# Four-layer graph network on one Trainium2 core: the order of work in the layer 0 edge loop

## The chip, the cores and the metric

The kernel runs on one core of one Trainium2 chip. Its time is the device time of one execution, in microseconds. The engines are TensorE (PE, with its weight loads as PEld), VectorE (DVE), ScalarE (ACT), GpSimd (POOL) and SyncE (SP). Each works through its own instructions in the order in which the program issues them, and waits for others by semaphores.

## The reference

Nodes N = 4096, features D = 512, edges E = 65536, everything in float32. Four layers follow each other; each one normalises the rows, takes the ReLU, lets a graph operation work on them and adds the result to x. The change lies in layer 0, an attention layer with 8 heads of 64 features over the set of distinct edges and self loops:

```python
h = jnp.einsum('nc,hcf->hnf', x, W)
e = s_src[:, :, None] + s_dst[:, None, :]      # one score of each node as source, one as destination
e = jnp.where(e > 0, e, ALPHA * e)
e = jnp.where(adj[None, :, :], e, NEG_INF)
att = jax.nn.softmax(e, axis=-1)
out = jnp.einsum('hij,hjf->hif', att, h)       # then concatenated over heads, softmax over axis 1
```

Layers 1 to 3 (a normalised sum over edges, a message network, another sum over edges) are not touched.

## The kernel before

Layer 0 first sorts the edges by source and projects all rows to `htab` (512 features and 8 scores per node). The function `attend` then walks over the sorted edges in `groups` = 64 groups of `GT` = 8 tiles of 128 edges. For every group it

- gathers 8 tiles of rows of `htab` with 8 indirect DMAs on POOL (`fetch`, three groups ahead, four buffers `rows`);
- makes one-hot matrices of the edges' sources on DVE (`one_hots`, line 414, one instruction for 8 tiles);
- turns these with 8 PE transposes into two PSUM tiles `t_ps` (`turn`, line 635), which ACT copies to `oh_t` (`turned`, line 643), while ACT (line 647) and DVE (line 648) blend the node parts of the two blocks that the group's sources can lie in into `of`;
- spreads these parts to the edges with 8 small PE products into `e_ps` (`source_parts`, line 656);
- makes the scores on DVE (`scores`, lines 662 to 668), their exponent on ACT (line 669), the weights on DVE (`weights`, line 676, into the PSUM tile `both_ps`) and a copy of the weights on ACT into the last columns of `rows` (line 677);
- weighs the rows pair by pair: 6 heads on DVE (`weigh`, line 690, one instruction for two tiles) and the last 2 heads on ACT (`weigh_last`, line 684, four instructions for two tiles);
- sums the weighed rows with the one-hots on PE (`add_up`, line 696; the trace shows 8 products for two tiles) into `sum_ps`, and one step later adds the sums to two blocks of `acc` on DVE (`keep`, line 431, two instructions).

The block numbers that `keep` and `turned` need are read into a register by the engine that uses them (`block_of`, line 425). In the trace such a read is a TENSOR_LOAD and a few register operations on the engine's sequencer (rows of "DVEq" and "ACTq").

Beside the groups run the blocks: when the sources have passed 128 nodes, the class `Block` finishes these rows (softmax, residual, layer norm, the product with layer 1's weights, line 408) in 13 small steps. `PLAN` says for each step how many groups after the block's end and at which named place of the loop it is issued. A block ends every two groups, so the steps of the loop alternate. In an odd step a block's `share`, `spread`, `variance`, `roots`, `sharpen`, `multiply` (8 PE products, line 408) and `put` are issued; in an even one `exponent` (ACT, line 730), `add` (DVE, lines 734 to 739), `normal`, `turn` (4 PE transposes, line 770), `turned` (ACT copy, line 774) and `store`.

PE, DVE, ACT and POOL keep the written order here (`tc.manual_schedule`), so the loop body below is each engine's queue. PSUM is full: two `sum_ps` of two banks, two `t_ps`, one `e_ps` and one `both_ps`. A group's two turned tiles and the block's turned tile or product share the two `t_ps` in turn.

Of the kernel before, what the change touches and what calls it, by code (L numbers as in the profile page):

```python
# [11 lines left out]
BF16 = mybir.dt.bfloat16  # L12
F32R = mybir.dt.float32r
I32 = mybir.dt.int32
AF = mybir.ActivationFunctionType
# [5 lines left out]
P = 128  # L21
# [13 lines left out]
def kernel(  # L35
# [23 lines left out]
    nc = tc.nc  # L59
    N, D = x.shape  # L60
    E, DE = edge_attr.shape
    H, _, F = w0.shape
# [45 lines left out]
    s_loc = src_pool.tile([P, W], F32, name="s_loc")  # L108
    s_new = src_pool.tile([P, W], F32, name="s_new")
    s_bi = src_pool.tile([1, 2, NW], I32, name="s_bi")  # L110
    s_half = src_pool.tile([P, 2, NW], F32, name="s_half")
# [299 lines left out]
    def one_hots(pool, loc, t0, n, bufs=None, ids=None, dtype=F32):  # L411

        oh = pool.tile([P, n, P], dtype, name="oh", bufs=bufs)
        nc.vector.tensor_tensor(oh, (row_i if ids is None else ids).unsqueeze(1).to_broadcast([P, n, P]),  # L414
                                loc[:, t0:t0 + n].unsqueeze(2).to_broadcast([P, n, P]), op=OP.is_equal)
        return oh
# [7 lines left out]
    def block_of(eng, bi, t):  # L424
        return eng.value_load(bi[:, t:t + 1], min_val=0, max_val=NB - 1)
# [163 lines left out]
    node3 = node_pool.tile([P, NB, 3, 2 * H], BF16, name="node3")  # L589
# [9 lines left out]
    GT = 8  # L599
# [4 lines left out]
    def attend(ctx):  # L604
        if True:
            ep = ctx.enter_context(tc.tile_pool(name="edge", bufs=2))
# [4 lines left out]
            ids_ps = both_ps[:, :P]  # L611
# [8 lines left out]
            def at(g):  # L620
                return g * GT
# [7 lines left out]
            def turn(oh):  # L629

                made = []
                for j in range(0, GT, 4):
                    t_ps = eps.tile([P, 4, P], F32, name="t_ps")
                    for k in range(4):
                        nc.tensor.transpose(t_ps[:, k, :], oh[:, j + k, :], ident)
                    made.append(t_ps)
                return made

            def turned(g, made):

                oh_t = ep.tile([P, GT, P], BF16, name="oh_t")
                for j, t_ps in enumerate(made):
                    nc.scalar.copy(oh_t[:, 4 * j:4 * j + 4, :], t_ps)
                of = ep.tile([P, 2, 3 * 2 * H], BF16, name="of")
                near = [node3[:, ds(block_of(e, s_bi[:, k, :], g), 1)].rearrange("p b k c -> p (b k c)")
                        for k, e in enumerate((nc.scalar, nc.vector))]
                nc.scalar.activation(of[:, 0, :], near[0], AF.Copy, scale=s_half[:, 0, g:g + 1])
                nc.vector.scalar_tensor_tensor(of[:, 1, :], near[1], s_half[:, 1, g:g + 1], of[:, 0, :],
                                               op0=OP.mult, op1=OP.add)
                return oh_t, of[:, 1, :]  # L650

            def source_parts(oh_t, of):

                e_ps = eps.tile([P, GT, 3, 2 * H], F32, name="e_ps", bufs=1)
                for j in range(GT):
                    nc.tensor.matmul(e_ps[:, j].rearrange("p k c -> p (k c)"), oh_t[:, j, :],
                                     of, start=True, stop=True)
                return e_ps

            def scores(rows, e_ps):  # L660
                near = ep.tile([P, GT, 2 * H], F32, name="near")
                nc.vector.reduce_sum(near, e_ps.rearrange("p t k c -> p t c k"), axis=AX.X)
                u = ep.tile([P, GT, H], F32, name="u")
                nc.vector.tensor_add(u, near[:, :, :H], rows[:, :, D:D + H])
                nc.vector.scalar_tensor_tensor(u, u, 0.2, u, op0=OP.mult, op1=OP.max)
                nc.vector.tensor_sub(u, u, near[:, :, H:])

                nc.vector.tensor_scalar(u, u, SAFE_RANGE + 10.0, None, op0=OP.min)
                nc.scalar.activation(u, u, AF.Exp)
                nc.scalar.copy(rows[:, :, D + H:], one2.unsqueeze(1).to_broadcast([P, GT, 2]))  # L670
                return u
# [7 lines left out]
            def weigh_last(j, rows):  # L679

                two = rows[:, j:j + 2]
                for k in range(2):
                    for h in range(VH, H):
                        nc.scalar.activation(two[:, k, h * F:(h + 1) * F], two[:, k, h * F:(h + 1) * F], AF.Copy,
                                             scale=two[:, k, D + h:D + h + 1])

            def weigh(g, j, rows):

                part = rows[:, j:j + 2, :VH * F].rearrange("p t (h f) -> p t h f", h=VH)
                nc.vector.tensor_mul(part, part,  # L690
                                     w_ps[:, g % 2, j:j + 2, :VH].unsqueeze(3).to_broadcast([P, 2, VH, F]))

            def add_up(j, rows, oh, ps):
                for k in range(2):
                    for c in range(2):
                        nc.tensor.matmul(ps[:, c, :HW], oh[:, j + k, :], rows[:, j + k, c * HW:(c + 1) * HW],  # L696
                                         start=j + k == 0, stop=j + k == GT - 1)
# [6 lines left out]
            class Block:  # L704
# [78 lines left out]
                def store(self):  # L783
                    nc.sync.dma_start(ytab[self.b * P:(self.b + 1) * P, :], self.row)

            PLAN = {"share": (0, "end"), "exponent": (1, "turned"), "add": (1, "end"), "spread": (2, "first"),
                    "variance": (2, "summed"), "roots": (2, "turned"), "sharpen": (2, "end"), "normal": (3, "first"),
                    "turn": (3, "between"), "turned": (3, "weighed"), "multiply": (4, "between"), "put": (4, "end"),
                    "store": (5, "summed")}
            begun = {}  # L790

            def blocks(g, place):

                for b in range(NB):
                    since = g - min(2 * b + 3, groups)
                    for step, when in PLAN.items():
                        if when == (since, place):
                            if step == "share":
                                begun[b] = Block(b)
                            getattr(begun[b], step)()  # L800
                            if step == "store":
                                del begun[b]

            rows, ohs, sums = {}, {}, {}
            for g in range(-3, groups + 6):
                now = lambda k: 0 <= k < groups
                if now(g + 3):
                    rows[g + 3] = fetch(g + 3)
                if now(g + 1):
                    made = turn(ohs[g + 1])  # L810
                if now(g):
                    sums[g] = eps.tile([P, 2, D], F32, name="sum_ps")
                    weigh(g, 0, rows[g])
                    add_up(0, rows[g], ohs[g], sums[g])
                    weigh_last(2, rows[g])
                    weigh(g, 2, rows[g])
                blocks(g, "first")
                if now(g - 1):
                    keep(g - 1, sums.pop(g - 1))
                    del rows[g - 1], ohs[g - 1]  # L820
                blocks(g, "summed")
                if now(g + 1):
                    parts = turned(g + 1, made)
                blocks(g, "turned")
                if now(g):
                    add_up(2, rows[g], ohs[g], sums[g])
                    weigh_last(4, rows[g])
                    weigh(g, 4, rows[g])
                if now(g + 2):
                    ohs[g + 2] = one_hots(ep, s_loc, at(g + 2), GT, 3, ids_ps)  # L830
                if now(g + 1):
                    e_ps = source_parts(*parts)
                if now(g):
                    add_up(4, rows[g], ohs[g], sums[g])
                blocks(g, "between")
                if now(g + 1):
                    u = scores(rows[g + 1], e_ps)
                if now(g):
                    weigh_last(6, rows[g])
                    weigh(g, 6, rows[g])  # L840
                blocks(g, "weighed")
                if now(g):
                    add_up(6, rows[g], ohs[g], sums[g])
                if now(g + 1):
                    weights(g + 1, rows[g + 1], u)
                    weigh_last(0, rows[g + 1])
                blocks(g, "end")

    one2 = node_pool.tile([P, 2], F32, name="one2")
    nc.vector.memset(one2, 1.0)  # L850
    attend()
    l0_pool.close()

# [173 lines left out]
    with tc.tile_pool(name="between", bufs=1) as bp, tc.tile_pool(name="between_ps", bufs=1, space=PSUM) as bps, \  # L1027
            tc.manual_schedule(engines=ENGINES):
        between = Between(bp, bps)
# [538 lines left out]
```

## Time and profile before

| | |
|---|---|
| time, median of 4 runs | 5419.7 us (5417.04 to 5427.41) |
| the profiled execution's own time | 5421.66 us |
| its span | 5419.9 us, granted TensorE clock 0.982 |
| PE, DVE, ACT, POOL busy over the span | 94%, 65%, 62%, 54% |
| layer 0 edge loop, first to last start of line 696 on PE | 256.7 to 926.6 us |
| one-hot instruction of one group (line 414, DVE) | 1.22 us, 64 of them |
| weigh instruction (line 690, DVE) | 0.95 us, 256 of them |

A row of a timeline is: start, duration, engine, line, operation, output and inputs, shape, number of instructions merged, and in brackets the idle time before the first of them with what ended it. Durations overlap on one engine, since the next instruction starts before the last one has drained, so the cost of an instruction in a full queue is the distance to the next start. A row of the waits is: who waited for whom, microseconds in total, times, the longest. A row of windows has the busy microseconds of PE, PEld, DVE, ACT and POOL with their instructions, the granted clock, the DMA share and the rate.

### The profile page before, as it was taken

The numbers are of one execution on the slowest core, as the hardware profiler recorded it, in microseconds if no ns is written. First come the engines' busy times: TensorE is split into PE (matmuls) and PEld (weight loads), VectorE is DVE, ScalarE is ACT, GpSimd is POOL, SyncE is SP. The second block draws the span as 40 slices with busy tenths as digits, with TensorE's granted clock in tenths as the row PEclk, the third lists the DMA queues.
The fourth block names the chain that finished last, engine by engine and source line by source line (L and its number), as shares of the span: only waits on it lengthen the run. The fifth ranks groups of instructions, "written<-read, shape, count | busy, mean of one in ns | idle before, by whom it ended". The sixth has DMA issues, their size and how long they took to land.

```text
span 5419.9 us, 56747 instructions
## 1 busy us (share of the span) xinstructions
PE 5093.7 (94%) x17274; PEld 2742.0 (51%) x17274; DVE 3526.8 (65%) x5843; ACT 3368.4 (62%) x5157; POOL 2910.4 (54%) x2604
## 2 busy tenths in 40 slices
PE   7799999799997999999999999999999899988887
PEld 4477776344443555555555555555555666522222
DVE  8689997333334777777777777777777466622333
ACT  1267776344445888888888888888888433333433
POOL 0177774777765555555555555555553111167776
PEclk9899999899998999999999999999999899999999
DMA  3388885888885555555555555555553211167787
GB/s 107 105 237 251 247 244 170 264 262 265 260 254 134 119 113 113 114 116 116 114 114 114 114 114 114 113 113 115 116 115 63 86 68 66 58 207 210 237 252 224
DMA packets 345929, 842.26 MB, mean 155 GB/s; under 512 B 61072, under 2 KB 77456, under 8 KB 345616
## 3 DMA queue, kind: packets, MB, share of 16 engines
q0 software_dynamic: 237568, 673.35, 50.0%
q1 hardware_dynamic: 108048, 165.19, 8.9%
q8 instruction: 141, 2.31, 0.2%
q14 instruction: 172, 1.41, 0.1%
HBM read 753.14 MB, written 85.20 MB: 155 GB/s over the span
## 4 chain that ended last, share of the span: by engine, by line
PE 77%; DMA 8%; POOL 6%; DVE 5%; issue 3%; ACT 1%; DVEq 0%; SPq 0%; POOLq 0%; ACTq 0%
PE m_ps L408 32%; PE sum_ps L887 9%; DMA g<-ztab,d_src 5%; PE small_ps L1084 4%; PE small_ps L1111 4%; PE o_ps L408 4%; PE tr_ps L1091 4%; PE sum_ps L696 4%; PE u_ps L1276 4%; PE pq_ps L985 4%; POOL g L419 4%; POOL rows L419 2%; DMA rows<-htab,s_dst 2%; PE t_ps L408 1%; PE tr_ps L1074 1%
## 5 line engine op out<-in xcount | busy, mean ns | idle before, releaser
L408 PE MATMUL m_ps<-w_sb,h_t 128*128 128x512 f32 x4096 | 1821.1, 592 | 0.5 <-ACT h_t L1093 0.5
L408 PEld LDWEIGHTS m_ps<-w_sb,h_t 128*128 128x128 f32 x4096 | 757.5, 190 | 809.6 <-issue 798.1
L887 PE MATMUL sum_ps<-g,oh 128*128 128x512 f32 x2048 | 1023.7, 617 | 143.7 <-DMA g<-ztab,d_src 92.5
L419 POOL DMA_INDIRECT pg<-ptab,d_src x512 | 497.6, 972 | 994.3 <-ACT h_t L1093 817.9
L1067 POOL DMA_INDIRECT pg<-qtab,d_dst x512 | 870.5, 1700 | 159.3 <-issue 153.2
L887 PEld LDWEIGHTS sum_ps<-g,oh 128*128 128x128 f32 x2048 | 357.7, 191 | 750.6 <-issue 343.3
L419 POOL DMA_INDIRECT rows<-htab,s_dst x512 | 491.9, 961 | 402.6 <-issue 371.2
L419 POOL DMA_INDIRECT g<-ztab,d_src x512 | 485.9, 949 | 240.7 <-issue 118.8
L419 POOL DMA_INDIRECT g<-ytab,s_dst x512 | 487.0, 951 | 234.1 <-issue 124.8
L1093 ACT COPY h_t<-tr_ps 128x512 f32<-128x512 f32 x512 | 275.2, 589 | 429.6 <-PE tr_ps L1091 429.4
L696 PE MATMUL sum_ps<-rows,oh 128*128 128x261 f32 x2048 | 495.1, 389 | 26.9 <-DVE rows L690 26.8
L431 DVE SCALAR_TENSOR_TENSOR acc<-sum_ps,d_half,acc 128x512 f32 x256 | 192.4, 751 | 444.0 <-PE sum_ps L887 418.5
L1143 DVE TENSOR_TENSOR pg<-pg,small_ps 128x512 f32<-128x512 f32 x512 | 318.3, 682 | 189.9 <-PE small_ps L1084 152.8
L696 PEld LDWEIGHTS sum_ps<-rows,oh 128*128 128x128 f32 x2048 | 376.6, 190 | 104.8 <-DVE rows L690 37.8
L431 DVE SCALAR_TENSOR_TENSOR acc<-sum_ps,s_half,acc 128x522 f32 (+1 forms) x256 | 193.1, 754 | 335.6 <-PE sum_ps L887 300.8
L1111 PE MATMUL small_ps<-parts,oh 128*128 128x512 f32 x1024 | 310.9, 446 | 13.4 <-DVE oh L414 13.4
L1105 DVE TENSOR_TENSOR parts<-z,parts 128x1024 fp32r<-128x1024 f32 x256 | 313.6, 1225 | 8.9
L1091 PEld LDWEIGHTS tr_ps<-ident,pg 128*128 128x128 f32 x2048 | 240.3, 141 | 145.5 <-issue 145.5
L1180 DVE TENSOR_TENSOR pg<-pg,qg 128x1024 f32<-128x1024 f32 x256 | 301.3, 1219 | 0.7 <-ACT qg L1177 0.7
L431 DVE SCALAR_TENSOR_TENSOR acc<-small_ps,d_half,acc 128x512 f32 x256 | 192.4, 752 | 161.4 <-PE small_ps L1111 152.5
L1267 POOL TENSOR_TENSOR h_sb<-h_sb,b_bc 128x1024 f32<-128x1024 f32 x16 | 38.1, 2382 | 453.9 <-PE tr L1251 430.2
L1091 PE MATMUL tr_ps<-ident,pg 128*128 128x128 f32 x2048 | 266.3, 273 | 10.4 <-DVE pg L1180 10.4
(281 smaller groups left out, 8047.7 us busy)
## 6 DMA issues: line engine op xcount, KB each, us to landing
eg<-in_edge_attr_dram SPq DMA_DIRECT2D x128, 128.0 KB, 2.6
xt<-in_x_dram SPq DMA_DIRECT2D x8, 1024.0 KB, 5.5
htab<-acc SPq DMA_DIRECT2D x32, 256.0 KB, 2.0
x_row<-in_x_dram SPq DMA_DIRECT2D x32, 256.0 KB, 4.3
rows<-htab,s_dst POOLq DMA_INDIRECT x512, 3.8
x<-x_row SPq DMA_DIRECT2D x32, 256.0 KB, 3.7
ytab<-acc SPq DMA_DIRECT2D x32, 256.0 KB, 4.4
x_mid<-x SPq DMA_DIRECT2D x32, 256.0 KB, 5.3
```

Source lines behind the costliest of these rows:

```text
L408: nc.tensor.matmul(ps, h_t[:, k, :], w_sb[:, k0 + k, :], start=start and k == 0, stop=stop and k == KC - 1)
L419: nc.gpsimd.indirect_dma_start(out=dst_ap, out_offset=None, in_=table, in_offset=bass.IndirectOffsetOnAxis(ap=idx, axis=0))
L431: nc.vector.scalar_tensor_tensor(at, ps, half[:, k, i:i + 1], at, op0=OP.mult, op1=OP.add)
L696: nc.tensor.matmul(ps[:, c, :HW], oh[:, j + k, :], rows[:, j + k, c * HW:(c + 1) * HW], start=j + k == 0, stop=j + k == GT - 1)
L887: nc.tensor.matmul(ps, oh[:, j, :], g[:, j, :], start=i % per == 0 and j == 0, stop=i % per == per - 1 and j == U - 1)
L1067: nc.gpsimd.indirect_dma_start(out=pg[:, j, :], out_offset=None, in_=qtab, in_offset=bass.IndirectOffsetOnAxis(ap=d_dst[:, t:t + 1], axis= ...
L1091: nc.tensor.transpose(h_ps[:, k, :], h[:, j, k * P:(k + 1) * P], ident)
L1093: nc.scalar.copy(h_t, h_ps)
L1105: nc.vector.tensor_sub(parts[:, 1], m, parts[:, 0].bitcast(F32))
L1111: nc.tensor.matmul(ps, oh[:, j, :], parts[j // 2][:, k, j % 2, :], start=j == 0 and k == 0, stop=j == U - 1 and k == 1)
L1143: nc.vector.tensor_add(nxt[:, j], nxt[:, j], ps)
L1180: nc.vector.tensor_mul(h[i][:, half], h[i][:, half], qg[:, half])
```

## The change

The one-hots are made, turned and copied two groups ahead instead of one, at the start of a step; the ACT half of the blend becomes a function of its own, issued before the copies; `source_parts` goes to the end of the step, two groups ahead. The first two pairs of the next group are weighed at the end of the step, the last two pairs of the group in its own step, so that `add_up(0)` and `add_up(2)` stand together at the start. `keep` goes behind the blocks' PE work. The one-hots get a fourth buffer. Two entries of `PLAN` move.

```diff
+            def near_scale(g):
+                of = ep.tile([P, 2, 3 * 2 * H], BF16, name="of")
+                near = node3[:, ds(block_of(nc.scalar, s_bi[:, 0, :], g), 1)].rearrange("p b k c -> p (b k c)")
+                nc.scalar.activation(of[:, 0, :], near, AF.Copy, scale=s_half[:, 0, g:g + 1])
+                return of
-            def turned(g, made):
+            def turned(g, made, of):
...
-                nc.scalar.activation(of[:, 0, :], near[0], AF.Copy, scale=s_half[:, 0, g:g + 1])
-                nc.vector.scalar_tensor_tensor(of[:, 1, :], near[1], s_half[:, 1, g:g + 1], of[:, 0, :],
+                near = node3[:, ds(block_of(nc.vector, s_bi[:, 1, :], g), 1)].rearrange("p b k c -> p (b k c)")
+                nc.vector.scalar_tensor_tensor(of[:, 1, :], near, s_half[:, 1, g:g + 1], of[:, 0, :],
...
-                    "variance": (2, "summed"), ... "turned": (3, "weighed"),
+                    "variance": (2, "weighed"), ... "turned": (3, "turned"),
...
-                if now(g + 1):
-                    made = turn(ohs[g + 1])
                 if now(g):
                     sums[g] = eps.tile([P, 2, D], F32, name="sum_ps")
-                    weigh(g, 0, rows[g])
                     add_up(0, rows[g], ohs[g], sums[g])
-                    weigh_last(2, rows[g])
-                    weigh(g, 2, rows[g])
+                    add_up(2, rows[g], ohs[g], sums[g])
+                    weigh_last(4, rows[g])
+                    weigh_last(6, rows[g])
                 blocks(g, "first")
+                if now(g + 2):
+                    ohs[g + 2] = one_hots(ep, s_loc, at(g + 2), GT, 4, ids_ps)
+                    made = turn(ohs[g + 2])
+                    of = near_scale(g + 2)
+                if now(g):
+                    weigh(g, 4, rows[g])
+                    add_up(4, rows[g], ohs[g], sums[g])
+                if now(g + 1):
+                    u = scores(rows[g + 1], e_ps.pop(g + 1))
+                if now(g):
+                    weigh(g, 6, rows[g])
+                blocks(g, "weighed")
+                if now(g + 2):
+                    parts = turned(g + 2, made, of)
+                blocks(g, "between")
+                blocks(g, "turned")
                 if now(g - 1):
                     keep(g - 1, sums.pop(g - 1))
                 blocks(g, "summed")
-                (from here: turned, "turned", add_up(2), weigh 4, one_hots(g + 2), source_parts(g + 1),
-                 add_up(4), "between", scores(g + 1), weigh 6, "weighed")
                 if now(g):
                     add_up(6, rows[g], ohs[g], sums[g])
                 if now(g + 1):
                     weights(g + 1, rows[g + 1], u)
-                    weigh_last(0, rows[g + 1])
+                    for j in (0, 2):
+                        weigh_last(j, rows[g + 1])
+                        weigh(g + 1, j, rows[g + 1])
+                if now(g + 2):
+                    e_ps[g + 2] = source_parts(*parts)
                 blocks(g, "end")
```

The three lines in brackets stand for the removed lines 822 to 841 of the kernel before.

More of the change, by code (lines that the diff above doesn't have):

```diff
@@ L643, in turned @@
                     nc.scalar.copy(oh_t[:, 4 * j:4 * j + 4, :], t_ps)
-                of = ep.tile([P, 2, 3 * 2 * H], BF16, name="of")
-                near = [node3[:, ds(block_of(e, s_bi[:, k, :], g), 1)].rearrange("p b k c -> p (b k c)")
-                        for k, e in enumerate((nc.scalar, nc.vector))]
-                nc.scalar.activation(of[:, 0, :], near[0], AF.Copy, scale=s_half[:, 0, g:g + 1])
-                nc.vector.scalar_tensor_tensor(of[:, 1, :], near[1], s_half[:, 1, g:g + 1], of[:, 0, :],
+                near = node3[:, ds(block_of(nc.vector, s_bi[:, 1, :], g), 1)].rearrange("p b k c -> p (b k c)")
+                nc.vector.scalar_tensor_tensor(of[:, 1, :], near, s_half[:, 1, g:g + 1], of[:, 0, :],
                                                op0=OP.mult, op1=OP.add)
@@ L786, in attend @@
             PLAN = {"share": (0, "end"), "exponent": (1, "turned"), "add": (1, "end"), "spread": (2, "first"),
-                    "variance": (2, "summed"), "roots": (2, "turned"), "sharpen": (2, "end"), "normal": (3, "first"),
-                    "turn": (3, "between"), "turned": (3, "weighed"), "multiply": (4, "between"), "put": (4, "end"),
+                    "variance": (2, "weighed"), "roots": (2, "turned"), "sharpen": (2, "end"), "normal": (3, "first"),
+                    "turn": (3, "between"), "turned": (3, "turned"), "multiply": (4, "between"), "put": (4, "end"),
                     "store": (5, "summed")}
@@ L802, in blocks @@
                                 del begun[b]
-            rows, ohs, sums = {}, {}, {}
+            rows, ohs, sums, e_ps = {}, {}, {}, {}
             for g in range(-3, groups + 6):
@@ L821, in attend @@
                 blocks(g, "summed")
[L822 to L841, printed above, removed]
                 if now(g):
```

## The prediction

> **What bounds the kernel now.** I read the page first, then the windows of the layer 0 loop, its waits, and the timelines of single steps. In the loop three engines are nearly full:
>
> ```profile
> 400.00:600.00 200.00, 197.46 (x1033) 154.50 (x1032) 184.21 (x402) 141.72 (x505) 151.78 (x159) 1.00 0.83 250
> ```
>
> PE is busy 98.7%, DVE 92% without its small gaps. POOL's 8 gathers of a group take 8 x 1.25 us (0.95 and 0.30 of issue, start to start) = 10.0 us. What PE does in an even step:
>
> ```profile
> 484.84 1.93 PE L696 MATMUL sum_ps<-rows,oh 128*128 128x261 f32 x8
> 486.61 1.03 PE L635 MATMUL t_ps<-ident,oh 128*128 128x128 f32 x8
> 487.48 3.70 PE L696 MATMUL sum_ps<-rows,oh 128*128 128x261 f32 x16
> 491.01 0.36 PE L656 MATMUL e_ps<-of,oh_t 128*128 128x48 bf16 x8
> 491.21 2.01 PE L696 MATMUL sum_ps<-rows,oh 128*128 128x261 f32 x8
> 493.06 0.60 PE L770 MATMUL t_ps<-ident,h_row 128*128 128x128 f32 x4
> 493.89 2.03 PE L696 MATMUL sum_ps<-rows,oh 128*128 128x261 f32 x8 [0.23 <-DVE rows L690]
> 495.76 0.49 PE L635 MATMUL t_ps<-ident,oh 128*128 128x128 f32 x3
> ```
>
> Starts give the prices: 8 products 1.77 us (484.84 to 486.61), the turn 0.87, 16 products 3.53, e_ps 0.20. The step lasts 9.15 us. The four transposes fill 0.44, so PE stands still from 493.50 to 493.89, and the first product after it costs 0.10 more: 0.5 us lost. The odd step before it runs from 474.87 to 486.61, 11.74 us with no gap. So the pair takes 20.9 us, its PE work 20.4, POOL's part 20.0. The waits of the steady stretch (320 to 895 us):
>
> ```profile
> DVE of L648 <- ACT root L752: 18.0, 27, 1.0
> POOL rows L419 <- PE sum_ps L696: 12.9, 17, 1.5
> PE sum_ps L696 <- DVE rows L690: 9.0, 31, 0.7
> DVE near L662 <- PE e_ps L656: 3.9, 21, 0.2
> ```
>
> PE waits for DVE, and DVE seems to wait for ACT at line 648. It does not. A register read stands in front of line 648; its TENSOR_LOAD begins when line 748 is issued, and from there to line 648 it takes 0.79 us, start to start, where line 748 by itself takes 0.13:
>
> ```profile
> 477.56 0.15 DVE L748 COPY var<-acc 128x1 f32<-128x1 f32 x1
> 478.35 0.27 DVE L648 SCALAR_TENSOR_TENSOR of<-node,s_half,of 128x48 bf16<-128x48 bf16 x1 [0.64 <-ACT root L752]
> ```
>
> The reads themselves, of the loop (min/median/max in ns):
>
> ```profile
> L425 DVEq TENSOR_LOAD <-s_bi x164: 296/306/973, 321.2 to 894.2; - x164
> L425 DVEq FUSED_REGOPS  x164: 190/190/190, 321.6 to 894.6; - x164
> ```
>
> So DVE's own queue sets the lap, and PE could gain 0.5 us in a pair at most.
>
> **The change part by part.** No work is added. PE's order moves 8 products, a turn and e_ps about; its sum stays 20.4.
>
> (a) *Fourth buffer of one-hots: 0.* No engine waits for a one-hot buffer: no row of these waits has line 414 on either side. The Trainium skill ("Perfetto Trace Analysis", Identifying Performance Opportunities) says that the same gap repeating on the engine that should be full can mean too few buffers; by that rule the repeated 0.5 us would come back here, about -13 us in all. The row says that this gap ends with line 690, not with a buffer.
>
> (b) *One-hots, turn and e_ps a group earlier.* Line 662's wait (0.19 per pair, 0.27 start to start) goes. PE's turn now stands behind a one-hot made in the same step: 1.22 us of DVE against 3.53 us of PE products ahead of it. DVE may be up to 2.3 us late against PE before PE waits; below I find 1.8 late in odd steps, 1.3 in even ones.
>
> (c) *Register reads.* On DVE the order is now scores, weigh 6, [variance], line 648, keep. Both reads (line 648's and keep's first) stand in a row behind line 668's issue: 0.79 as above and 0.83 with keep's extra register operation, 1.62 to line 431. They are covered by line 668 (0.15), weigh 6 (0.87), line 648 (0.19) and in odd steps the variance (0.24). Exposed: 0.4 in the even, 0.2 in the odd step; bounds 0 and, with the slowest read of the row (973 against 306 ns), 0.67 more. The gaps before line 648 (0.64 and 0.10) go. I take the median, since 141 of the 164 reads are under 350 ns in the trace. The skill's page "DMA: Bandwidth & Descriptors" (Latency and other measured facts) gives a tensor load a floor of about 600 ns; by it each read would be 0.3 longer, the pair 1.2 and the loop some 30 us. The measured 306 ns decides.
>
> (d) *Weights, then at once weigh 0.* This is the new wait. Line 690's first instruction does not only need line 676 of its own engine; it waits for ACT's copy of the weights, line 677. In the full loop that is hidden, since `add` or `sharpen` and `share` lie between. Step 1, before there are blocks, shows it bare:
>
> ```profile
> 264.65 0.95 DVE L690 TENSOR_TENSOR rows<-rows,both_ps 128x768 f32<-128x768 f32 x1
> 265.70 0.23 DVE L676 TENSOR_TENSOR both_ps<-u,s_new 128x64 f32<-128x64 f32 x1
> 266.21 0.95 DVE L690 TENSOR_TENSOR rows<-rows,both_ps 128x768 f32<-128x768 f32 x1 [0.28 <-ACT rows L677]
> ```
>
> and ACT in the same microsecond:
>
> ```profile
> 265.99 0.19 ACT L677 COPY rows<-both_ps 128x64 f32<-128x64 f32 x1
> ```
>
> Line 676 to line 690 costs 0.51 instead of 0.14 in every step, if ACT is free. In even steps it is not. Its queue is now: copies to `oh_t`, then the block's copy (line 774), which waits for PE's four transposes, then `exponent` (line 730), and only then line 677. Behind the waiting line 690 on DVE stand weigh 2 and `add`; PE's next `add_up(0)` waits for it.
>
> The path in an even step, from PE's first product: 16 products 3.6 (with 0.07 of start-up), turn 0.87, 8 products 1.77 = 6.25; transposes to result 0.60; ACT 0.03 + line 774 0.47 + line 730 0.71 + line 677 0.19; line 690 0.03 + 0.95; PE 0.05. Sum 9.28. PE's own work in the step is 8.65, so a wait of 0.63 takes the place of the 0.5. Odd steps: 0.07 + 3.53 + 0.87 + 1.77 + 3.43 + 1.77 + 0.20 = 11.65 to the 11.74 of now. Pair: 20.93 to 21.02, I take 21.0.
>
> DVE's own lap: 20.90 - 0.64 - 0.10 - 0.27 (line 662) - 2 x 0.18 (line 676 no longer right behind line 690: 1.05 against 0.87) + 2 x 0.37 (d) + 0.6 (c) = 20.9. The two laps are equal, so DVE has no cover left: what a read costs more goes to the end.
>
> (e) *ACT half of the blend earlier, weigh_last 4 and 6 first, keep later: 0.* ACT has 14.8 us of work in 20.9, and its read moves behind `spread` or `normal` (0.71 us, covering 0.64). keep must end before the next step's first product on the same `sum_ps`: 8.3 us into the step, of 9.3 or 11.7. In odd steps the `oh_t` copy must end before `multiply` takes its PSUM tile: 6.25 us against 6.25; between 0 and 0.1 per pair, taken as 0.
>
> (f) *Start and end.* While gathers pace the loop (to group 9), the way from landing to PE's first product was 324.77 (line 664) to 329.41, 4.64; now 0.78 + 1.62 + 1.47 (keep) + 0.51 + 0.95 + 0.05 = 5.38: +0.7. At the end group 62 has no turn: 8.66 becomes 8.4, -0.3.
>
> **Sum.** 26 pairs from group 9 to 61 x 0.1 = +2.6, with (f) +3.0. On the profiled 5421.7 this gives 5424.7, on the median (2.0 lower) 5422.7. The layers behind shift with the loop's end.
>
> **The rivals.** *Slower: DVE becomes the bound through its register reads.* For it: about one read in each pair takes 0.4 to 0.97 us now, hidden under weigh 2; in the new order nothing hides it. From a lap of 21.0 on it decides; 0.67 more makes 21.57, 26 x 0.67 + 0.4 = +18, 5438. With the mean of the slow reads (0.65) it would be 21.25, +9.5. Against it: the slow ones come when a store has just been issued, and the reads now stand elsewhere.
>
> *Faster: line 677 comes early enough*, so that PE runs without a gap: 26 x -0.5 + 0.4 = -13, 5407. This needs ACT 0.6 us earlier in even steps, which nothing in the queue gives, or no wait at line 690; step 1 shows that wait.
>
> *The order does nothing:* POOL's 20.0 us and jitter keep the lap at 20.9, 5420. Against it: POOL itself waits 12.9 us for PE.
>
> **How the numbers follow.** 0.2% is 10.8 us, about what a measurement of this kernel can tell from no change. The new wait: 0.53 (-2 to +10). Reads as bound: 0.29, of which 0.27 over +10.8. Cover found: 0.13. Nothing moves: 0.05. So faster 0.13, same 0.60, slower 0.27. The likeliest case alone spans 5418 to 5430 in time; with the bounds of the reads and most of the gain the range is 5408 to 5437.
>
> **What would show it.** Right: PE's gap sits before the first `add_up(0)` after an even step, some 0.6 us, ended by line 690; line 690 shows waits for ACT line 677; line 648 has no gap and line 431 has one of 0.2 to 0.4; the pair takes 21.0. Wrong: the pair at 20.4 with PE gapless, or DVE at 21.3 and more with PE waiting in odd steps also, or one-hot or `t_ps` waits in front of PE's turn.

## The result and the profile after

The change made the kernel slower by a little: 5428.65 us (median of 32 runs, 5423.16 to 5433.3) against 5420.9 us (52 runs, 5415.81 to 5428.32), a ratio of 1.0014 with a 95% interval of 1.0009 to 1.0019. The prediction said 5422.7, 0.11% less, with the range 5408 to 5437. The profiled execution took 5431.3 us, with a span of 5429.4 us at a granted clock of 0.983. Most lines of `attend` have moved by four: 676, 677, 690, 696, 730, 770 and 774 of before are 680, 681, 694, 700, 734, 774 and 778 now; 643 and 648 are 650 and 652, and the scores, 662 to 668, are 666 to 672.

The window of the layer 0 loop that was shown of before, now with PE busy 2.5 us less in it (PE, PEld, DVE, ACT, POOL, granted clock, DMA share, GB/s):

```profile
400.00:600.00 200.00, 195.01 (x1021) 151.42 (x1020) 180.43 (x396) 139.58 (x497) 147.50 (x156) 1.00 0.82 243
```

The timeline of an even step after:

```profile
467.97 3.78 PE L700 MATMUL sum_ps<-rows,oh 128*128 128x261 f32 x16
...
471.58 1.04 PE L635 MATMUL t_ps<-ident,oh 128*128 128x128 f32 x8
...
472.46 1.93 PE L700 MATMUL sum_ps<-rows,oh 128*128 128x261 f32 x8
...
474.09 1.58 DVE L431 SCALAR_TENSOR_TENSOR acc<-sum_ps,s_half,acc 128x522 f32 x2 [0.38 <-issue]
474.23 0.60 PE L774 MATMUL t_ps<-ident,h_row 128*128 128x128 f32 x4
474.66 1.93 PE L700 MATMUL sum_ps<-rows,oh 128*128 128x261 f32 x8
474.86 0.59 ACT L778 COPY h_row_t<-t_ps 128x512 f32<-128x512 f32 x1 [0.69 <-PE t_ps L774]
475.35 0.72 ACT L734 ACTIVATE h_row<-h_row,low 128x512 f32<-128x512 f32 x1
475.58 0.29 DVE L680 TENSOR_TENSOR both_ps<-u,s_new 128x64 f32<-128x64 f32 x1
...
476.06 0.20 ACT L681 COPY rows<-both_ps 128x64 f32<-128x64 f32 x1
476.30 1.82 DVE L694 TENSOR_TENSOR rows<-rows,both_ps 128x768 f32<-128x768 f32 x2 [0.43 <-ACT rows L681]
476.43 0.36 PE L660 MATMUL e_ps<-of,oh_t 128*128 128x48 bf16 x8
477.31 1.37 PE L700 MATMUL sum_ps<-rows,oh 128*128 128x261 f32 x5 [0.51 <-DVE rows L694]
```

PE's gap has moved. The 8 products of `add_up(6)` follow the block's four transposes without a wait (474.23 to 474.66), and PE now stops after `e_ps`, ahead of the next `add_up(0)`, until line 694 is done. The path to it reads from start to start: ACT had the block copy (474.86), which waited for PE's transposes, then the exponent (475.35), and only then the copy of the weights (476.06); line 694 followed at 476.30 and PE at 477.31. DVE was hardly earlier: line 680 ended at 475.87, so ACT held the copy up by 0.19 us. The waits of the same stretch as before (320 to 895 us; total, times, longest):

```profile
PE sum_ps L700 <- DVE rows L694: 16.3, 27, 1.0
DVE rows L694 <- ACT rows L681: 16.2, 54, 0.5
DVE acc L431 <- issue: 10.9, 27, 0.7
DVE acc L431 <- DVE of L652: 9.6, 27, 0.7
PEld t_ps L408 <- ACT oh_t L650: 7.3, 27, 0.5
```

PE waited 9.0 us for DVE in this stretch before, and 16.3 now, once in each pair and always after the even step. Line 694 waits for ACT 54 times, twice in a pair. The wait of line 648 is gone, and `keep` (line 431) has two new ones of 0.40 and 0.36 us on average, behind the register reads.

In the table the times are from PE's first product of one group to that of the next. Only the steady part, groups 9 to 61 (26 pairs), enters the mean.

| | before | predicted | after |
|---|---|---|---|
| even step | 9.16 | 9.28 | 9.34 to group 22, 9.40 later |
| odd step | 11.74 | 11.65 to 11.74 | 11.95 to group 22, 11.76 later |
| pair, mean | 20.98 | 0.1 more | 21.24 |
| group 0 to group 9 | 93.67 | 0.7 more | 95.04 |
| group 61 to the last product | 30.78 | 0.3 less | 30.82 |
| whole loop | 669.9 | 3.0 more | 678.0 |

26 x 0.26 + 1.4 = 8.1 us in the loop, beside the 7.75 between the medians.

### The profile page after: what moved, and what is told of

It is laid out like the page before. It is cut to its first block, busy times and chain, and to the rows that moved or that the text cites. A ratio compares the mean times of both kernels' runs of the same rounds, so it can differ in the third digit from the quotient of the medians.

```text
span 5429.4 us, 56745 instructions
## 1 busy us (share of the span) xinstructions
PE 5091.9 (94%) x17274; PEld 2736.6 (50%) x17274; DVE 3521.2 (65%) x5843; ACT 3370.9 (62%) x5157; POOL 2919.8 (54%) x2604
## 4 chain that ended last, share of the span: by engine, by line
PE 76%; DMA 9%; POOL 5%; DVE 4%; issue 3%; ACT 2%; DVEq 0%; ACTq 0%; SPq 0%; POOLq 0%
PE m_ps L408 32%; PE sum_ps L889 10%; DMA g<-ztab,d_src 6%; PE small_ps L1086 4%; PE small_ps L1113 4%; PE o_ps L408 4%; PE tr_ps L1093 4%; PE u_ps L1278 4%; PE pq_ps L987 4%; PE sum_ps L700 4%; POOL g L419 3%; DMA rows<-htab,s_dst 2%; POOL rows L419 2%; PE t_ps L408 1%; PE tr_ps L1076 1%
```

## The experiments

The theory: in the kernel after, two laps of nearly equal length set the pair. One is ACT's chain in the even step (block copy, exponent, copy of the weights, line 694), the other is DVE's own queue with its exposed register reads. Rivals: one of the two alone is the bound; or POOL's pace and jitter are, whatever the order. The last of these falls below: the pair came down to 20.33 with the gathers, 20.0 us of a pair, untouched. A second question is what made the gap in the kernel before. Times are medians; each ratio is against the kernel before in the same series.

| kernel | time, us | before beside it | ratio, 95% interval | pair, us |
|---|---|---|---|---|
| after | 5428.65 | 5420.9 | 1.0014, 1.0009 to 1.0019 | 21.24 |
| weights by DVE | 5410.21 | 5419.53 | 0.9983, 0.9974 to 0.9992 | 20.61 |
| exponent first | 5426.03 | 5419.53 | 1.0011, 1.0002 to 1.002 | 21.17 |
| reads ahead | 5425.05 | 5419.53 | 1.001, 1.0001 to 1.0019 | 21.14 |
| exponent and reads | 5407.22 | 5421.46 | 0.9972, 0.9961 to 0.9983 | 20.46 |
| all three | 5403.15 | 5422.52 | 0.9963, 0.995 to 0.9977 | 20.33 |
| before, read ahead | 5416.42 | 5419.53 | 0.9993, 0.9984 to 1.0002 | 20.86 |
| before, and DVE's weigh 6 ahead | 5433.05 | 5422.52 | 1.0021, 1.0012 to 1.003 | 21.36 |
| before, and both halves ahead | 5410.49 | 5421.46 | 0.9977, 0.9968 to 0.9987 | 20.51 |

### The copy of the weights made by DVE

```diff
-                nc.scalar.copy(rows[:, :, D:D + H], w)
+                nc.vector.tensor_mul(rows[:, :, D:D + H], u, s_new[:, at(g):at(g) + GT].unsqueeze(2).to_broadcast([P, GT, H]))
```

DVE writes the weights a second time, straight into `rows`, and ACT's copy is gone.

> The changed kernel, with ScalarE's copy of the weights into the rows (line 681 of the changed kernel) replaced by a second multiplication on VectorE that writes them there. So weigh's first instruction has nothing of ScalarE's to wait for. Theory (the wait on the copy behind exponent holds TensorE up in even steps, and VectorE's own lap is as long): line 680 to weigh 0 goes from 0.50 to about 0.3 in both steps, weigh 0 is no longer tied to exponent, the pair goes from 21.2 to about 20.75: 26 x -0.45 = -12 against the changed kernel, some 5417 us. Rival 1 (register reads on VectorE alone are the cause): they stay, but so does VectorE's gain of 0.4 a pair minus 0.3 for the second multiplication: -3, 5426. Rival 2 (one-hots, turn and copies two groups ahead are the cause): no change, 5428 to 5429.

The timeline of the weights in an even step of this kernel, and two rows of its waits (320 to 895 us):

```profile
471.62 0.23 DVE L680 TENSOR_TENSOR both_ps<-u,s_new 128x64 f32<-128x64 f32 x1
471.75 0.22 DVE L681 TENSOR_TENSOR rows<-u,s_new 128x64 f32<-128x64 f32 x1
471.88 1.81 DVE L694 TENSOR_TENSOR rows<-rows,both_ps 128x768 f32<-128x768 f32 x2
```

```profile
DVE acc L431 <- issue: 11.4, 28, 0.7
PE sum_ps L700 <- DVE rows L694: 2.3, 7, 0.7
```

From the weights to line 694 it is now 0.26 us, against 0.72 in the step shown above, and PE's 16.3 us of waiting have shrunk to 2.3. The gaps of `keep` are as before (11.4 us). The time is 5410.21 us, more gained than expected: 26 x 0.63 = 16.4 us in the pairs instead of 12, and 1.7 at the start and end of the loop. So without the copy PE has back what it lost. But this edit does not tell the two laps apart, since it shortens both: ACT's chain no longer reaches line 694, and DVE is rid of the copy's bare price in each step, 0.28 us as the next kernel shows, for the 0.13 of the second product.

### One lap at a time: exponent first, reads ahead

```diff
-            PLAN = {..., "exponent": (1, "turned"), ...
+            PLAN = {..., "exponent": (1, "first"), ...
```

> The changed kernel with one entry of PLAN moved: exponent from (1, turned) to (1, first), so that ScalarE does it before the copies to oh_t and the copy of the weights is 0.71 us earlier in its queue in even steps. Theory with two equal laps: the ScalarE path loses 0.7, but VectorE's lap of some 21.1 remains, so only the stretch with odd steps of 11.95 gains: -1 to -4, 5425 to 5428. Rival (the path through ScalarE is the only cause): even steps go from 9.38 to 8.7, 26 x -0.65 = -17, 5412.

In the other kernel both reads go ahead of work that can cover them: that of line 652 ahead of the one-hots, `keep`'s first behind weigh 4, each handed on as a register.

```diff
+                    at_1 = block_of(nc.vector, s_bi[:, 1, :], g + 2)
                     made = turn(ohs[g + 2])
...
                     add_up(4, rows[g], ohs[g], sums[g])
+                if now(g - 1):
+                    at_0 = block_of(nc.vector, s_bi[:, 0, :], g - 1)
```

> The changed kernel with two of the three register reads of VectorE in a step issued earlier: the one for the blend behind the one-hots, the first one of keep behind weigh 4, where instructions of 1.1 and 0.9 us cover them. Theory with two equal laps: line 431's idle time of 0.33 and 0.38 goes, VectorE's lap falls to some 20.45, but the path through ScalarE (even step 9.3) stays: pair 21.0 to 21.1, 26 x -0.15 = -4, 5424 to 5426. Rival (the register reads are the only cause): 20.45 to 20.5, 26 x -0.75 = -19, 5409.

Rows of the waits, first of the exponent's kernel, then of the reads':

```profile
PE sum_ps L700 <- DVE rows L694: 15.7, 27, 0.9
DVE rows L694 <- ACT rows L681: 15.1, 54, 0.3
DVE acc L431 <- issue: 10.9, 27, 0.7
```

```profile
DVE rows L694 <- ACT rows L681: 43.4, 54, 1.6
PE sum_ps L700 <- DVE rows L694: 14.8, 28, 0.9
```

Both gained little, 2.6 and 3.6 us beside the kernel after, as the theory said (1 to 4), and their ratios cannot be told from its 1.0014. With ACT relieved, line 694 waits 0.28 on average, the bare price of the copy, and PE waits as long as ever: DVE's queue is the bound (steps of 9.38 and 11.76). With DVE relieved, `keep`'s gaps are gone from the rows, and the time comes back at line 694, whose waits for ACT rise from 16.2 to 43.4 us: ACT's chain is the bound, with a median even step of 9.34. The two laps are 21.1 each.

### Both laps, and all three edits

> The kernel after with the exponent earlier on ACT and both register reads ahead on DVE, a second time, since the first chip granted a clock of 0.95 only. Theory (two laps of nearly equal length, ACT's chain to the copy of the weights and DVE's queue with its reads): the pair falls from 21.24 to 20.4 to 20.7, 5408 to 5413. Rival (the copy of the weights bounds the step by itself, 0.28 us before line 694 in each): 21.1 to 21.2, 5424 to 5427.

> The kernel after with the weights' second product on DVE, the exponent earlier and the reads ahead, a second time, for the same reason. At a clock of 0.98, theory (PE is the bound, its waits gone): even step 8.65 to 8.7, odd 11.7, pair 20.4, 5406 to 5409. Rival (DVE with 0.23 more work per step becomes the bound): 5411 to 5416.

With the exponent and the reads together the time is 5407.22 us and the pair 20.46, although the copy of the weights and its wait are still there. That settles the two laps: each alone hides behind the other. It also rules out the copy as a bound by itself. With all three edits PE has no gap in the steady loop:

```profile
400.00:600.00 200.00, 200.00 (x1070) 158.71 (x1070) 188.39 (x438) 144.81 (x506) 151.39 (x160) 1.00 0.84 252
```

The steps are 8.67 and 11.66, which is the sum of PE's own work, 20.33. This version, at 5403.15 us (5399.93 to 5404.96, 5 runs), beats both kernels. It is about 3 us under the lower end of what was expected; the kernel with two of the edits is 1 us under.

### What made the gap in the kernel before

First the register read of line 648 alone, issued ahead of `keep` in the kernel before and handed on to `turned`:

```diff
+                if now(g + 1):
+                    at_1 = block_of(nc.vector, s_bi[:, 1, :], g + 1)
                 if now(g - 1):
                     keep(g - 1, sums.pop(g - 1))
```

> The kernel before with one register read moved: VectorE's read for the blend (line 648) is issued ahead of keep's two reads. Theory (the 0.64 us in front of line 648 are the register read and not a wait for ScalarE, and VectorE's lap sets the pair): this idle time goes, VectorE's lap falls from 20.9 to 20.2, TensorE's 20.4 to 20.5 becomes the bound: 27 x -0.45 = -12 against the kernel before, 5408 to 5410. Rival (line 648 waits for ScalarE's root, as the list of waits has it): the gap stays and the time with it, 5420 to 5421.

Neither number came out. Most of the idle time in front of line 648 went: 18.0 us in the loop before, put down to ACT's root, and now

```profile
DVE of L648 <- ACT of L647: 6.3, 24, 0.4
```

So the gap was mainly the register read; behind it stood a shorter wait, for ACT's half of the blend (line 647), which shows in 24 steps. The odd step fell from 11.74 to 11.66. But the even step stayed at 9.2. Its timeline:

```profile
594.44 0.36 PE L656 MATMUL e_ps<-of,oh_t 128*128 128x48 bf16 x8
594.64 2.01 PE L696 MATMUL sum_ps<-rows,oh 128*128 128x261 f32 x8
594.84 0.56 DVE L662 TENSOR_REDUCE near<-e_ps 128x128 f32<-128x384 f32 x1 [0.43 <-PE e_ps L656]
...
596.32 0.95 DVE L690 TENSOR_TENSOR rows<-rows,both_ps 128x768 f32<-128x768 f32 x1
596.49 0.60 PE L770 MATMUL t_ps<-ident,h_row 128*128 128x128 f32 x4
597.32 2.03 PE L696 MATMUL sum_ps<-rows,oh 128*128 128x261 f32 x8 [0.23 <-DVE rows L690]
```

DVE is early now and idles 0.43 us until PE's `e_ps`. Behind that stand the scores and only then weigh 6, which PE's `add_up(6)` needs. The chain starts on PE itself, so reaching line 662 still earlier on DVE cannot shorten it; another order can. A first attempt moved DVE's weigh 6 ahead of `scores`, with the read still ahead:

```diff
+                if now(g):
+                    weigh(g, 6, rows[g])
                 if now(g + 1):
                     u = scores(rows[g + 1], e_ps)
                 if now(g):
                     weigh_last(6, rows[g])
-                    weigh(g, 6, rows[g])
```

> The kernel before with line 648's register read ahead of keep and DVE's weigh 6 ahead of scores, a second time: the first time the chip granted a clock of 0.95 and the loop had stalls of some 4 us that none of the kernels shows elsewhere, so nothing of 0.1% could be read. At a clock of 0.98, theory (the chain e_ps, scores, weigh 6, add_up(6) makes the gap of the even step): pair 20.4 to 20.5, 5406 to 5409. Rival (DVE's whole lap): pair 20.86, 5416 to 5418. Second rival (later weights delay weigh 0 and the gap moves to add_up(0)): 5418 to 5424.

It came out slower than every case written down, at 5433.05 us. The edit had a flaw. Its timeline in an even step:

```profile
603.83 0.26 ACT L669 ACTIVATE u<-u 128x64 f32<-128x64 f32 x1 [3.25 <-DVE u L668]
...
604.09 1.06 ACT L684 ACTIVATE rows<-rows 128x64 f32<-128x64 f32 x4
...
604.72 1.59 PE L696 MATMUL sum_ps<-rows,oh 128*128 128x261 f32 x6 [0.60 <-ACT rows L684]
```

ACT's half of weigh 6 had stayed behind the exponent of the scores, which came later, and ACT had idled 3.25 us there. PE now waited 0.60 for ACT instead of 0.23 for DVE. The second attempt moves both halves ahead of `scores` (shown against the first):

```diff
                 if now(g):
+                    weigh_last(6, rows[g])
                     weigh(g, 6, rows[g])
                 if now(g + 1):
                     u = scores(rows[g + 1], e_ps)
-                if now(g):
-                    weigh_last(6, rows[g])
```

> The kernel before with line 648's register read ahead of keep and both halves of weigh 6, DVE's and ACT's weigh_last, ahead of scores. In the run with DVE's half alone, add_up(6) of the even step waited 0.60 us for ACT's half, which had stayed behind scores' exponent. Theory (the even step's gap in the kernel before is the chain e_ps, scores, weigh 6, add_up(6)): the gap before add_up(6) is gone; of the 0.5 us some 0.3 come back before add_up(0), since the weights are 0.6 us later and weigh 0 ends some 0.3 us after PE's turn: even step 8.7 to 9.0, odd 11.66 to 11.7, pair 20.4 to 20.7, 5406 to 5414. Rival (DVE's whole lap sets the pair): 20.86 as with the read alone, 5416 to 5418. Second rival (the weights' delay costs more than the gap): 5422 and above.

The same place in the timeline of this kernel, and PE's wait for weigh in its loop (320 to 895 us):

```profile
592.38 0.60 PE L770 MATMUL t_ps<-ident,h_row 128*128 128x128 f32 x4
...
592.81 1.93 PE L696 MATMUL sum_ps<-rows,oh 128*128 128x261 f32 x8
...
594.58 1.03 PE L635 MATMUL t_ps<-ident,oh 128*128 128x128 f32 x8
```

```profile
PE sum_ps L696 <- DVE rows L690: 0.4, 2, 0.2
```

PE's wait has shrunk from 9.0 to 0.4 us, the median even step is 8.67 and the pair 20.51: 26 x -0.47 = -12, beside a measured -11.0. So the even step's gap of before was the chain from `e_ps` over the scores to weigh 6; the register read cost 0.12 of a pair (20.98 to 20.86). Both can be mended in the old order, one group ahead, with three buffers of one-hots. The new place of weigh 6 without the earlier read was not run.

### Four runs on a slower chip

Four kernels ran first on a chip where the kernel before took 5805.45 us (35 runs), at a granted clock of 0.95: the kernel after with three buffers of one-hots, and the first runs of three kernels already told of. Of the kernel after itself there is no run on that chip.

```diff
-                    ohs[g + 2] = one_hots(ep, s_loc, at(g + 2), GT, 4, ids_ps)
+                    ohs[g + 2] = one_hots(ep, s_loc, at(g + 2), GT, 3, ids_ps)
```

> The kernel after with three buffers of one-hots as before. The one-hots of g + 2 then take the buffer of g - 1, whose last product was issued at the end of the step before. Theory (the fourth buffer is worth nothing in the full loop): DVE's line 414 comes some 3 us after PE's last product of g - 1, so no wait: 5427 to 5430. Rival (the fourth buffer is a part of what the order needs): DVE waits for PE at line 414 by 0.3 us or more in each step, pair 21.6 or more, 5438 and above.

> The kernel before with line 648's register read ahead of keep (as in the run before this one) and DVE's weigh 6 issued ahead of scores instead of behind it. Theory (in the kernel before PE's gap in even steps comes from the chain e_ps, scores, weigh 6, add_up(6): DVE idles 0.43 us before line 662 and has weigh 6 ready behind it): even step 9.16 to 8.75, odd 11.66, pair 20.4 to 20.5, 26 x -0.5 = -13 against before: 5406 to 5409. Rival (DVE's whole lap sets the step, whatever the order): pair 20.86 as with the read alone, 5416 to 5418. Second rival (scores 0.5 later makes the weights and so weigh 0 of the next step late): the gap moves to add_up(0), 5418 to 5424.

> The kernel after with the exponent in an earlier place on ACT (as e2) and both register reads on DVE issued ahead (as e3); alone each changed nothing. Theory (two laps of nearly equal length: ACT's chain to the copy of the weights, and DVE's own queue with its reads): only both together shorten the pair, from 21.24 to 20.6, 26 x -0.65 = -17: 5411 to 5413. Rival (the copy of the weights, line 681, bounds the step by itself, since each step still pays 0.28 us before line 694): pair stays at 21.1 to 21.2, 5424 to 5427.

> The kernel after with the weights' second product on DVE instead of ACT's copy (e1), the exponent earlier (e2) and the reads ahead (e3). Theory (with the copy gone PE is already nearly the bound; the other two take away the last of its waits): even step 8.65 to 8.7, odd 11.7, pair 20.4, 0.1 less than with e1 alone: 5406 to 5409. Rival (DVE has more work by 0.23 per step and becomes the bound again): 5411 to 5416.

The ratios were 1.0035 (1.0014 to 1.0056) with three buffers, 0.9998 (0.9978 to 1.0018) with DVE's weigh 6 ahead, 0.9969 (0.9947 to 0.999) with exponent and reads, and 0.9955 (0.9935 to 0.9975) with all three. The granted clock in the loop (320 to 895 us) was 0.89 to 0.95 there, against 1.00 above, and steps took from 8.7 to 27 us. Signs agree with the later runs for the last two, sizes cannot be read, and the first attempt at weigh 6 showed nothing. The three buffers are inconclusive too. On that chip DVE did wait for PE in front of the one-hots, which it did not once in the kernel after at full clock (waits of 300 to 1150 us):

```profile
DVE oh L414 <- PE sum_ps L700: 12.2, 8, 1.8
```

In the kernel after at full clock, groups 20 to 39, the one-hots begin 1.2 to 2.7 us after the last product that reads the buffer of three groups earlier. That argues that three buffers cost nothing there, with less slack than the 3 us of the expectation; it was not measured.

## Why the prediction was right, and where it was off

**The new wait, step (d): right, with its place.** Gap, releaser and queue are those forecast. The path of the even step, added up from the timeline of after: 16 products 3.61, turn 0.88, 8 products 1.77, to the block copy 0.63, to the exponent 0.49, to the copy of the weights 0.71, to line 694 0.24, to PE 1.01, together 9.34; the forecast was 9.28. Taking away the copy gave PE its time back, and so did clearing the way to it once DVE's reads were moved too, so the cause is shown: this path together with DVE's lap, neither alone. The pair, 21.24, lies between the sign of being right (21.0) and that of being wrong (21.3 and more).

**DVE's lap, steps (c) and (d): right that it has no cover left, 0.2 too short.** It was 20.9 in the forecast; with ACT out of the way it measured 21.14. Part of that is the odd step, where reads were exposed by 0.36 instead of 0.2; the even step's 0.40 was right. The rest, 0.08, is open. The faster rival asked for ACT to be 0.6 us earlier; the kernel with the exponent first gave it that, and DVE's lap kept the time at 5426.03. From group 23 on this lap, not ACT's, ends last: line 681 follows line 680 at once, as the timeline of after shows (the last line belongs to the odd step behind it and is used below).

```profile
602.54 0.72 ACT L734 ACTIVATE h_row<-h_row,low 128x512 f32<-128x512 f32 x1
603.16 0.22 DVE L680 TENSOR_TENSOR both_ps<-u,s_new 128x64 f32<-128x64 f32 x1
...
603.41 0.21 ACT L681 COPY rows<-both_ps 128x64 f32<-128x64 f32 x1
...
609.81 0.20 DVE L672 TENSOR_SCALAR u<-u 128x64 f32<-128x64 f32 x1
```

**The rival of slow reads: DVE did become the bound, but not through slow reads.** From a lap of 21.0 on, the rival said, DVE decides; the lap was 21.14, and from group 23 on it does. But no read in the loop after took over 332 ns (min/median/max, on DVE's sequencer):

```profile
L425 DVEq TENSOR_LOAD <-s_bi x162: 297/304/332, 323.9 to 887.5; - x162
```

The bound of 0.67 came from a row of the old order, where up to 973 ns were seen, and did not carry over. (Of the 164 reads in that row 140 took under 350 ns; the forecast has 141.) The Trainium skill ("DMA: Bandwidth & Descriptors", Latency and other measured facts) gives a floor of about 600 ns for a tensor load; by the forecast's estimate that would have made the loop 30 us longer. The median of 304 ns here decides against it again.

**The odd step, step (e): this term was mis-sized.** The forecast set 6.25 against 6.25 and took the difference as 0. In groups 10 to 22 `multiply` waits 0.19 for the `oh_t` copy, as the timeline of after shows:

```profile
460.50 1.93 PE L700 MATMUL sum_ps<-rows,oh 128*128 128x261 f32 x8
...
461.14 0.41 DVE L672 TENSOR_SCALAR u<-u 128x64 f32<-128x64 f32 x1
...
462.46 3.70 PE L408 MATMUL t_ps<-w_sb,h_row_t 128*128 128x512 f32 x8
```

8 products begin 1.77 us before the next work, so `multiply` could have started at 462.27. The copies stand behind the scores' exponent on ACT, and line 672, the last of the scores, took 0.41 instead of the usual 0.20. From group 23 on it takes 0.20 in every odd step (as at 609.81 above), and the odd step falls from 11.95 to 11.76. The tie had no slack, and 0.2 of lateness went straight to PE. The traces of four kernels agree on this: after, weights by DVE, exponent first and reads ahead. From group 9 to 61 they have 21 odd steps in which line 672 took 0.28 us or more, and these lasted 11.85 to 12.00; of the other 83, all but one lasted 11.75 to 11.77. With the exponent first, line 672 was short in groups 12 to 18, and the odd steps there took 11.75 to 11.76 where after took 11.94 to 12.00. No run changed it alone.

**Start and end, step (f).** +1.4 instead of +0.7, and 0.0 instead of -0.3; not followed further. The start differs between the kernels in any case, from 93.4 to 95.1 us.

**The fourth buffer, step (a).** The Trainium skill ("Perfetto Trace Analysis", Identifying Performance Opportunities) says that a gap repeating on the engine that should be saturated can mean too few buffers. Read as in the forecast, it would have had the gap closed here by the fourth buffer. With the fourth buffer the gap only moved, and the kernel before lost it by order alone, with three. The row that named line 690 was the better guide.

**What bounded the kernel before: only half right.** "DVE's own queue sets the lap" holds for the read, not for the even step's gap. The 0.19 in front of line 662, put down as a small wait that the change removes, was the start of the chain that held PE. This did not spoil the forecast, since the change cut that chain and put another of about the same length in its place. But the statement that PE could gain 0.5 at most was a little low: 20.98 to 20.33 is 0.65. (The forecast's 20.9 was one pair; the mean of the 26 is 20.98.)

The sum, then: the mechanism was right, and the loop cost 8.1 instead of 3.0. Of the 5.1 between them the pair's 0.16 is 4.2, the start 0.7 and the end 0.3. That the time stayed so near the old one is chance as far as the order goes: a gap of 0.5 went and one of 0.6 came.

## What to carry to other kernels

When a step is moved up against its consumer, write out the queue of every engine on the way, since the copy that was hidden before is now behind whatever stands there; if a step is split over two engines, move both halves. Where two laps are equal, shortening one measures as next to nothing (2.6 and 3.6 us here, 21.4 together), so test both together before giving up either. An idle gap named after another engine can be for the most part the engine's own register read: look at its sequencer and try the read earlier.

## What the runs showed of the hardware

A small DVE instruction seems to be held to the end of a gather's issue. In the kernel after, line 672 takes 0.195 us in 40 of 54 steps and 0.28 to 0.42 in 14. All of these 14 began 0.55 to 0.69 us after a POOL gather (line 419) had begun, and ended 15 to 23 ns after that gather's end; none of the others, which began at another point of a gather or beside none, took over 0.2. In the three other kernels named above 21 more took 0.28 us or longer; all began 0.55 to 0.73 us into a gather and ended 15 to 23 ns after it, and no short one began there. This is an association in four traces, not an experiment. In the kernel after it recurs in each odd step of groups 10 to 22, where PE is 0.2 us late.

The kernel before took 5419.5 to 5422.5 us on three chips (a granted clock of 0.98) and 5805 us on a fourth (0.95); what slowed the fourth is open. A change of 0.1% can only be read against the kernel before on the same chip, and the fourth, with 5771 to 5824 us, spread too far for it.
